# State copies moved from GpSimd to ScalarE, products written one column beside the scan, and one more unit on GpSimd

## The chip, the cores and the metric

The kernel runs on one core of one Trainium2 chip. The time is device time in microseconds (us) for the whole program. A core has five engines that each work through their own queue in order: TensorE (PE, matrix products), VectorE (DVE), ScalarE (ACT), GpSimd (POOL) and SyncE (SP, which here only starts DMA transfers). They wait for each other by semaphores, so an instruction that waits holds up all that stands behind it on its engine.

## The reference, cut to what matters

Two layers work on 8 images of 64 channels and 128 x 128 pixels. The first is an adaptive 3 x 3 filter. The second is a block with two bidirectional selective scans (Mamba) and a convolutional feed-forward part. The scans carry this change. For one direction of one block, in the reference's terms:

```
dt  = softplus(dt)
dA  = exp(einsum('bdl,dn->bldn', dt, A))          # 128 channels d, 16 states n
dBu = einsum('bdl,bnl,bdl->bldn', dt, Bm, u)
h[l] = dA[l] * h[l-1] + dBu[l]                    # along the 16384 pixels l
y   = einsum('bldn,bnl->bdl', h, Cm) + D * u
```

Each image runs it four times: block 0 forward, block 0 backward, block 1 backward, block 1 forward.

## The kernel before, in words

**Chunks and units.** The 16384 pixels are cut into 16 chunks of T = 1024. An image is four passes of 16 chunks (forward, backward, backward, forward; `d` is 0 for forward and 1 for backward), so 512 chunks in all. The first pass over a block (passes 1 and 3 of an image, `second` false) stores its y to memory; the second pass (2 and 4, `second` true) adds that y, multiplies by the gate and projects. A chunk has 128 channels x 16 states = 2048 rows, that is U = 16 units of 128 rows. Units go in pairs k = 0 to 7, unit u = 2k + i.

**What one unit costs each engine.** ScalarE makes the decay `w = exp(...)` in PSUM (`decay`, L1194; two buffers, so unit u takes the buffer of unit u-2). GpSimd makes the drive `bu` for a pair at a time (`drive`, L1186, 2048 columns, four buffers). VectorE runs `tensor_tensor_scan` (`scan`, L1212 forward, L1214 backward, the latter with all operands reversed). Its start value is one column of `state`, 16 columns that hold the last h of every unit. Then h is multiplied by C (`product`), the last h is kept in `state` for the next chunk, and TensorE sums each pair over the states into one PSUM bank `y` (`collect`, L1244 to L1251).

**Who multiplies.** `on_pool(u)` decides. It holds for even units but 4 and 12, so for u = 0, 2, 6, 8, 10, 14; a unit that meets a block of GELUs on ScalarE (`gelu_times`, 112 times in the program, always unit 6 or 14) is left out. For these units the scan writes into the SBUF tile `hs`, GpSimd copies the last column to `state` (L1231) and then multiplies in place (L1232). For the other units the scan writes over `w`, VectorE multiplies into `hs` (L1235) and ScalarE copies the last column of `w` to `state` (L1236). `hs` has four buffers of two units.

**Order.** Nothing is scheduled automatically. `plan` puts every call at a time step (one step is one scan, b is the chunk's first) and a phase (FEED, SCAN, MID, PROD, EXP, DECAY, REST), and the calls are made in that order; each engine's queue follows. The scan of unit u is at b+u, a product on VectorE at b+u PROD, one on GpSimd at b+u+1 FEED, the decay of unit u at b+u-2 EXP, the drive of pair k at b+2k-5 REST, the sum of pair k at b+2k+3 REST (one later for k = 0 and 4). In a first pass the `y` bank is copied out by ScalarE (`y_out`, L1268) at b+8h+11 DECAY for h = 0 and 1, and stored by SP (`store_y`, L1271) a step later; the next sum that needs the bank is at b+12 REST (k = 4) or at the next chunk's b+4 REST (k = 0).

**Work of other stages** is spread over the same steps: the adaptive filter of the next image (Front: `weight` L594, `weighted` L598, `softmax` L567 and L575) from about the fourth chunk of pass 3 through pass 4, a mixing stage (`times` L815, `plus` L818) through the first 11 chunks of pass 1, the feed-forward part (L892, L898, L946 to L956) from there through pass 2 into pass 3. The first image has its own filter beside its pass 1, the last has no next image's filter but its own mixing and feed-forward at the end.

Of the kernel before, what the change touches and what calls it, by code (L numbers as in the profile page):

```python
# [8 lines left out]
F32 = mybir.dt.float32  # L9
BF16 = mybir.dt.bfloat16  # L10
AF = mybir.ActivationFunctionType
ALU = mybir.AluOpType
# [3 lines left out]
P = 128  # L16
# [14 lines left out]
T = 1024  # L31
# [3 lines left out]
U = G * G  # L35
PW = W + 2
FEED, SCAN, MID, PROD, EXP, DECAY, REST = range(7)
# [18 lines left out]
def kernel(ctx: ExitStack, tc: tile.TileContext, a: dict, out: bass.AP):  # L56
# [6 lines left out]
    nc = tc.nc  # L63
# [124 lines left out]
    with tc.tile_pool(name="wspill", bufs=1) as fp, tc.tile_pool(name="wprep", bufs=2) as pp, \  # L188
            tc.tile_pool(name="wps", bufs=4, space=PSUM) as pps:
        with tc.manual_schedule():  # L190
# [106 lines left out]
            for k in range(9):  # L297
                i, j = divmod(k, 3)
# [23 lines left out]
            for (g, c0, r0, n), fn, fdn in parts:  # L322
# [7 lines left out]
                for k in range(9):  # L330
                    i, j = divmod(k, 3)
# [22 lines left out]
            for l in range(DEPTH):  # L354
# [9 lines left out]
                for d in range(2):  # L364
                    cw, xdt, xbc, dtn, al, dp = dirs[2 * l + d]
                    taps = by_taps(inx2, cw, DI, KC)
                    for j in range(KC):
                        t = turned(taps[:, j, :], ident, P, DI)
                        at = j if d == 0 else KC - 1 - j
# [39 lines left out]
    def at(time, phase, fn, *args):  # L409
        steps.setdefault((time, phase), []).append((fn, args))  # L410

    inp = ctx.enter_context(tc.tile_pool(name="in", bufs=2))
    wk = ctx.enter_context(tc.tile_pool(name="wk", bufs=2))
# [442 lines left out]
    class Ffn:  # L856
# [57 lines left out]
                    )  # L914

        def before_taps_out(self):
            self.pre = wk.tile([P, 2, T], F32, tag="hs", name="f1", bufs=4)
            for i, bank in enumerate(self.banks):
                lo = 3 * PW * (i % 2)
                nc.scalar.copy(self.pre[:, i // 2, lo : lo + 3 * PW], bank[:, 0 : 3 * PW])  # L920
# [99 lines left out]
    gelu_times = {IMAGE * b + FFN_AT + FFN_STEP * c + GELU for b in range(B - 1) for c in range(NCH)}  # L1020
# [7 lines left out]
    class Chunk:  # L1028


        def __init__(self, i):
            self.b, self.l, self.d, self.t, self.second = order[i]
            self.i, self.t0 = i, U * i
            self.first = i % NT == 0
            self.pairs = PAIRS[i % 2]
            r, last = self.t0 % IMAGE, self.b == B - 1
            self.beside_front = (
                FRONT_AT - FRONT_STEP <= r < FRONT_AT + NCH * FRONT_STEP + 16 and not last
            ) or self.t0 < FIRST_FRONT_AT + (NCH - ALONE) * FRONT_STEP + 16
            self.prev = None  # L1040
            self.bus, self.hss, self.ws = {}, {}, {}
            self.dup, self.dtp, self.bp, self.cp, self.yv = {}, {}, {}, {}, {}
            self.norm = Norm()

# [127 lines left out]
        def on_pool(self, u):  # L1172


            if u % 2 or u % 8 == 4 or self.t0 + u - 1 in gelu_times:
                return False
            return True

        def over_pair(self, what, k):
            j = self.pairs[k][0]  # L1180
# [18 lines left out]
        def scan(self, u):  # L1199
            k, i = divmod(u, 2)  # L1200
            if u == 0:
                if self.first:
                    self.state = wk.tile([P, U], F32, tag="state", name="state")
                    nc.vector.memset(self.state, 0.0)
                else:
                    self.state = self.prev.state
            if i == 0:
                self.hss[k] = wk.tile([P, 2, T], F32, tag="hs", name="hs", bufs=4)
            w, hs, bu, s0 = self.ws.pop(u), self.hss[k][:, i, :], self.bus[k][:, i, :], self.column(u)
            to = hs if self.on_pool(u) else w  # L1210
            if self.d == 0:
                nc.vector.tensor_tensor_scan(to, w, bu, s0, ALU.mult, ALU.add)  # L1212
            else:
                nc.vector.tensor_tensor_scan(to[:, ::-1], w[:, ::-1], bu[:, ::-1], s0, ALU.mult, ALU.add)  # L1214
            if not self.on_pool(u):
                self.ws[u] = w

        def column(self, u):
            (j, gp), i = self.pairs[u // 2], u % 2
# [5 lines left out]

        def product(self, u):
            k, i = divmod(u, 2)
            j, hs = self.pairs[k][0], self.hss[k][:, i, :]
            c = self.cp[j // 2][:, j % 2, :]
            if self.on_pool(u):  # L1230
                nc.gpsimd.tensor_copy(self.column(u), self.last(hs))  # L1231
                nc.gpsimd.tensor_tensor(hs, hs, c, ALU.mult)  # L1232
            else:
                w = self.ws.pop(u)
                nc.vector.tensor_tensor(hs, w, c, ALU.mult)  # L1235
                nc.scalar.copy(self.column(u), self.last(w))  # L1236

        def collect(self, k):

            hs, gp = self.hss.pop(k), self.pairs[k][1]  # L1240
            if k % 4 == 0:
                self.y = py.tile([P, N], F32, tag="y", name="y")
                for h, s in enumerate(halves):
                    nc.tensor.matmul(  # L1244
                        self.y[C * h : C * h + C, :], dskip[:, self.l, self.d, C * gp : C * gp + C], self.xc[:, s],
                        start=True, stop=False,
                    )
            for h, s in enumerate(halves):
                for i in range(2):
                    lo = C * h + 32 * i  # L1250
                    nc.tensor.matmul(  # L1251
                        self.y[lo : lo + 32, :], sel_y, hs[:, i, s], start=False, stop=(k % 4 == 3)
                    )
# [58 lines left out]
        def plan(self):  # L1312
            b = self.t0 - 2 * U

            def feed(t, fn, *args):
                if self.beside_front:
                    at(t, FEED, fn, *args)
                else:
                    at(t - 1, REST, fn, *args)

            at(b + 3, REST, self.load_hn)
            for h in range(2):
                feed(b + 7 + h, self.conv, h)
                at(b + 7 + h, DECAY, self.conv_out, h)
                if self.second:
                    feed(b + 9 + h, self.gate, h)
                    at(b + 9 + h, DECAY, self.gate_out, h)
                feed(b + 14 + h, self.step, h)
                at(b + 14 + h, DECAY, self.step_out, h)
            at(b + SILU, REST, self.silu)  # L1330
            at(b + SOFTPLUS, REST, self.softplus)
            if self.second:
                at(b + 13, REST, self.store_gate)
            b = self.t0
            feed(b - 16, self.bc)
            at(b - 16, DECAY, self.bc_out)
            at(b - 14, REST, self.store_bc)
            at(b - 13, REST, self.store_dt)
            at(b - 11, FEED, self.dtx)
            at(b - 10, REST, self.store_du)  # L1340
            j0 = self.pairs[0][0] // 2
            at(b - 10, REST, self.load_states, "bp", j0)
            at(b - 8, REST, self.load_channels, "dup", 0)
            at(b - 6, REST, self.load_channels, "dtp", 0)
            at(b - 5, REST, self.load_states, "bp", 1 - j0)
            at(b - 4, REST, self.load_states, "cp", j0)
            at(b - 3, REST, self.load_channels, "dup", 1)
            at(b - 2, REST, self.load_channels, "dtp", 1)
            at(b - 1, REST, self.load_states, "cp", 1 - j0)
            for k in range(U // 2):  # L1350
                at(b + 2 * k - 5, REST, self.drive, k)
                at(b + 2 * k + 3 + (k % 4 == 0), REST, self.collect, k)
            for u in range(U):
                at(b + u - 2, EXP, self.decay, u)
                at(b + u, SCAN, self.scan, u)
                at(b + u + self.on_pool(u), FEED if self.on_pool(u) else PROD, self.product, u)
            for h in range(2):
                if self.second:
                    at(b + 8 * h + 1, REST, self.load_yf, h)
                    at(b + 8 * h + 6, REST, self.add_yf)  # L1360
                    at(b + 8 * h + 7, REST, self.load_gate, h)
                if self.second:
                    at(b + 8 * h + 11, MID, self.y_out, h)
                else:
                    at(b + 8 * h + 11, DECAY, self.y_out, h)
                    at(b + 8 * h + 12, REST, self.store_y, h)
            if not self.second:
                return
            b += U
            n = self.norm  # L1370
            at(b + 2, REST, self.load_h)
            feed(b + 5, self.project)
            at(b + 6, DECAY, self.residual)
            at(b + 6, DECAY, self.square)
            if self.l == 0:
                at(b + 7, REST, self.store_h)
            feed(b + 12, lambda: n.means(mm_tile, self.sq))
            at(b + 13, DECAY, n.means_out)
            feed(b + 17, n.spread, mm_tile)
            at(b + 19, MID, self.normed)  # L1380
            if self.l:
                at(b + 20, DECAY, self.weighted)
            at(b + 20, REST, self.store_hn)
# [48 lines left out]
```

## Time and profile before

| | |
|---|---|
| median of 3 runs | 28777.77 us (28775.38 to 28782.68) |
| the profiled execution, its own time | 28791.63 us |
| its span on the page | 28789.8 us, mean granted TensorE clock 0.874 |
| scans on VectorE | 8192 of 2344 ns |
| drives on GpSimd | 4096 of 4534 ns |
| products on GpSimd / on VectorE | 2960 of 2352 ns / 5232 of 1222 ns |
| state copies on GpSimd / on ScalarE | 2960 of 186 ns / 5232 of 158 ns |
| du on GpSimd (L1142) | 512 of 2361 ns |

All further numbers are from this one profiled execution. Durations overlap a little from one instruction to the next, so where the text needs what an instruction really takes of its engine, it uses the distance from its start to the next start in the timeline. A memset of `state` (L1204) stands at the first scan of each pass, so its 32 starts cut the span into 32 passes: the third image's passes run from 7429 to 8293, 9150, 10012 and 10920 us, the first image's from 405 to 1285, 2144, 3014 and 3928 us, the last two passes of all from 26643 to 27487 and 28358 us.

### The profile page before, as it was taken

What the parts mean: (1) busy time and instruction counts of PE and PEld (TensorE: products, weight loads), DVE (VectorE), ACT (ScalarE), POOL (GpSimd) and SP (SyncE); (2) the same over time, 40 slices, a digit from 0 to 9 for tenths busy, and PEclk for the clock granted to TensorE, in tenths of its full rate; (3) what the DMA queues carried; (4) which work ended last, traced back from release to release, by engine and by line L of the source; (5) the groups of instructions that cost most, each with busy time, mean ns of one, the idle gap of its engine ahead of it and who ended that gap; (6) DMA issues with size and microseconds to landing.
All of it is one profiled execution on the core that took longest, in us unless ns stands there. A gap on an engine that the chain in (4) does not pass through costs nothing. (4 is left out here: it accounts for less than half of the span.)

```text
span 28789.8 us, 311790 instructions
## 1 busy us (share of the span) xinstructions
PE 22950.3 (80%) x97708; PEld 7231.1 (25%) x97708; DVE 27022.6 (94%) x17438; ACT 18537.2 (64%) x26170; POOL 27203.7 (94%) x11052
## 2 busy tenths in 40 slices
PE   7666888878788787887878788787887878878578
PEld 3112322223222232222322222222222222222123
DVE  6999999999999999999999999999999999999997
ACT  4666666666666666666666666666666666666663
POOL 4999999999999999999999999999999999999993
PEclk7777889989899888998989888898888988889789
DMA  5777787777877678776777777777777777777674
GB/s 157 226 237 222 237 254 239 247 224 238 257 238 249 223 235 259 239 243 227 241 251 244 234 233 245 245 249 231 233 250 239 252 226 236 251 240 251 203 249 140
DMA packets 2592499, 6762.78 MB, mean 235 GB/s; under 512 B 431494, under 2 KB 737046, under 8 KB 2589686
## 3 DMA queue, kind: packets, MB, share of 16 engines
q1 hardware_dynamic: 2589958, 6742.69, 72.4%
q8 instruction: 774, 12.68, 0.2%
q14 instruction: 887, 7.27, 0.1%
q10 hardware_dynamic: 880, 0.14, 0.0%
HBM read 5509.49 MB, written 1265.19 MB: 235 GB/s over the span
## 5 line engine op out<-in xcount | busy, mean ns | idle before, releaser
L1186 POOL TENSOR_TENSOR bu<-dup,bp 128x2048 f32<-128x2048 f32 x4096 | 18545.7, 4534 | 30.2 <-DMA hn_dram<-hn 11.6
L1194 ACT ACTIVATE w<-dtp,a_neg 128x1024 f32<-128x1024 f32 x8192 | 9159.5, 1119 | 1621.1 <-DVE hs L1214 704.6
L1232 POOL TENSOR_TENSOR hs<-hs,cp 128x1024 f32<-128x1024 f32 x2960 | 6963.0, 2352 | 250.9 <-DMA cp<-bc_dram 12.6
L1235 DVE TENSOR_TENSOR hs<-w,cp 128x1024 f32<-128x1024 f32 x5232 | 6394.6, 1222 | 302.3 <-DMA cp<-bc_dram 127.2
L1214 DVE TENSOR_TENSOR_SCAN w<-w,state,bu 128x1024 f32<-128x1024 f32 x2651 | 6214.8, 2344 | 119.7 <-ACT w L1194 92.4
L1212 DVE TENSOR_TENSOR_SCAN w<-w,state,bu 128x1024 f32<-128x1024 f32 x2581 | 6052.5, 2345 | 176.0 <-ACT w L1194 145.9
L1251 PE MATMUL y<-hs,sel_y 128*32 128x512 f32 x32768 | 4976.6, 687 | 678.1 <-POOL hs L1232 677.1
L1236 ACT COPY state<-w 128x1 f32<-128x1 f32 x5232 | 828.3, 158 | 5555.8 <-DVE hs L1235 5494.1
L1212 DVE TENSOR_TENSOR_SCAN hs<-w,state,bu 128x1024 f32<-128x1024 f32 x1515 | 3549.7, 2343 | 171.1 <-ACT state L1236 68.6
L1214 DVE TENSOR_TENSOR_SCAN hs<-w,state,bu 128x1024 f32<-128x1024 f32 x1445 | 3385.7, 2343 | 145.9 <-ACT state L1236 68.6
L1061 PE MATMUL xp<-hn,wx 128*128 128x512 f32 x4096 | 2345.9, 701 | 780.0 <-ACT xc L1067 317.3
L892 PE MATMUL fp<-fw,bgw 128*128 128x512 f32 (+1 forms) x5760 | 2196.4, 625 | 222.7 <-DMA fw<-xn_dram 214.6
L1244 PE MATMUL y<-xc,dskip 128*64 128x512 f32 x4096 | 1445.3, 792 | 1109.9 <-ACT yv L1268 955.9
L1103 PE MATMUL dp<-xc,wdt 128*128 128x512 f32 x2048 | 1322.7, 732 | 586.6 <-ACT dt L1110 267.6
L1251 PEld LDWEIGHTS y<-hs,sel_y 128*32 128x32 f32 x32768 | 715.4, 115 | 4228.9 <-issue 2387.4
L68 ACT ACT_TABLE_LOAD x1137 | 1458.8, 1283 | 20.8 <-PEq L1421 0.7
L1067 ACT ACTIVATE xc<-xp,cbias 128x512 f32<-128x512 f32 x1024 | 697.7, 681 | 1180.2 <-PE xp L1061 1176.3
L898 PE MATMUL fp<-fw,bgw 64*128 64x512 f32 (+1 forms) x5760 | 1383.4, 607 | 0.0
L1061 PEld LDWEIGHTS xp<-hn,wx 128*128 128x128 f32 x4096 | 799.8, 213 | 2192.5 <-issue 878.2
L609 PE MATMUL acc<-t,ident 128*128 128x512 f32 x2160 | 1332.8, 705 | 0.7 <-DVE t L598 0.7
L1142 POOL TENSOR_TENSOR du<-dt,xc 128x1024 f32<-128x1024 f32 x512 | 1208.7, 2361 | 49.6 <-ACT dt L1116 49.6
L594 PE MATMUL wb<-wt,sel_k 65*128 65x512 bf16 x1152 | 502.0, 437 | 909.4 <-DVE t L598 782.1
(211 smaller groups left out, 24911.1 us busy)
## 6 DMA issues: line engine op xcount, KB each, us to landing
bp<-bc_dram SPq DMA_DIRECT2D x4096, 256.0 KB, 3.9
dup<-du_dram SPq DMA_DIRECT2D x4096, 256.0 KB, 5.2
dtp<-dt_dram SPq DMA_DIRECT2D x4096, 256.0 KB, 5.1
cp<-bc_dram SPq DMA_DIRECT2D x4096, 256.0 KB, 4.8
hn<-hn_dram SPq DMA_DIRECT2D x1024, 256.5 KB, 4.5
dt_dram<-dt SPq DMA_DIRECT2D x512, 512.0 KB, 2.9
du_dram<-du SPq DMA_DIRECT2D x512, 512.0 KB, 2.6
yf_dram<-yv SPq DMA_DIRECT2D x512, 256.0 KB, 4.6
```

The lines of the kernel that those rows point to most:

```text
L68: nc.scalar.preload_act_table_set("natural_log_exp_and_others")
L892: nc.tensor.matmul(o, wpair[:, i, g, m], self.win[h][:, i : i + ROWS, 0:W], start=(i == 0), stop=False)
L898: nc.tensor.matmul(o, wlast[rows, i, g, m], self.win[h][rows, i : i + ROWS, lo : W + lo], start=False, stop=(i == 2),)
L1061: nc.tensor.matmul(self.xp[h], wx[:, self.l, self.d, i, :], self.hn2[:, s.start + 2 * i : s.stop + 2 * i], start=(i == 0), stop=(i == 1),)
L1186: nc.gpsimd.tensor_tensor(bu, self.dup[self.pairs[k][1]], self.over_pair("bp", k), ALU.mult)
L1194: nc.scalar.activation(w, self.dtp[gp][:, i, :], AF.Exp, scale=a_neg[:, self.l, self.d, g, j : j + 1])
L1212: nc.vector.tensor_tensor_scan(to, w, bu, s0, ALU.mult, ALU.add)
L1214: nc.vector.tensor_tensor_scan(to[:, ::-1], w[:, ::-1], bu[:, ::-1], s0, ALU.mult, ALU.add)
L1232: nc.gpsimd.tensor_tensor(hs, hs, c, ALU.mult)
L1235: nc.vector.tensor_tensor(hs, w, c, ALU.mult)
L1244: nc.tensor.matmul(self.y[C * h : C * h + C, :], dskip[:, self.l, self.d, C * gp : C * gp + C], self.xc[:, s], start=True, stop=False,)
L1251: nc.tensor.matmul(self.y[lo : lo + 32, :], sel_y, hs[:, i, s], start=False, stop=(k % 4 == 3))
```

## The change

The tile `hs` gets one column more (T + 1). On GpSimd's units the scan writes columns 1 to T in a forward pass and 0 to T-1 in a backward one; the product goes to columns 0 to T-1 or 1 to T, so it is in place but one column beside. The column with the last h is not overwritten, and ScalarE copies it to `state` (`keep`) where GpSimd did. In backward passes the product on GpSimd has all operands reversed, as the scan has. `on_pool` gives GpSimd unit 12 also, in first passes only. There the copy and the store of `y` move one step later.

```diff
-            if u % 2 or u % 8 == 4 or self.t0 + u - 1 in gelu_times:
+            if u % 2 or u == 4 or self.t0 + u - 1 in gelu_times:
                 return False
-            return True
+            return u != 12 or not self.second
...
-                self.hss[k] = wk.tile([P, 2, T], F32, tag="hs", name="hs", bufs=4)
-            w, hs, bu, s0 = self.ws.pop(u), self.hss[k][:, i, :], self.bus[k][:, i, :], self.column(u)
-            to = hs if self.on_pool(u) else w
+                self.hss[k] = wk.tile([P, 2, T + 1], F32, tag="hs", name="hs", bufs=4)
+            w, bu, s0 = self.ws.pop(u), self.bus[k][:, i, :], self.column(u)
+            to = self.hss[k][:, i, 1 - self.d : 1 - self.d + T] if self.on_pool(u) else w
+            self.hs[u] = to
...
         def product(self, u):
             k, i = divmod(u, 2)
-            j, hs = self.pairs[k][0], self.hss[k][:, i, :]
-            c = self.cp[j // 2][:, j % 2, :]
-            if self.on_pool(u):
-                nc.gpsimd.tensor_copy(self.column(u), self.last(hs))
-                nc.gpsimd.tensor_tensor(hs, hs, c, ALU.mult)
+            j = self.pairs[k][0]
+            out, hs, c = self.hss[k][:, i, self.d : self.d + T], self.hs[u], self.cp[j // 2][:, j % 2, :]
+            if not self.on_pool(u):
+                nc.vector.tensor_tensor(out, hs, c, ALU.mult)
+            elif self.d == 0:
+                nc.gpsimd.tensor_tensor(out, hs, c, ALU.mult)
             else:
-                w = self.ws.pop(u)
-                nc.vector.tensor_tensor(hs, w, c, ALU.mult)
-                nc.scalar.copy(self.column(u), self.last(w))
+                nc.gpsimd.tensor_tensor(out[:, ::-1], hs[:, ::-1], c[:, ::-1], ALU.mult)
+
+        def keep(self, u):
+            nc.scalar.copy(self.column(u), self.last(self.hs.pop(u)))
...
+            for u in range(U):
+                at(b + u + self.on_pool(u), EXP if self.on_pool(u) else PROD, self.keep, u)
...
-                    at(b + 8 * h + 11, DECAY, self.y_out, h)
-                    at(b + 8 * h + 12, REST, self.store_y, h)
+                    at(b + 8 * h + 12, DECAY, self.y_out, h)
+                    at(b + 8 * h + 13, REST, self.store_y, h)
```

`collect` reads `hs` at the shifted columns, and the feed-forward tile that shares the `hs` buffers is declared one column longer; nothing else changes.

More of the change, by code (lines that the diff above doesn't have):

```diff
@@ L916, in before_taps_out @@
         def before_taps_out(self):
-            self.pre = wk.tile([P, 2, T], F32, tag="hs", name="f1", bufs=4)
+            self.pre = wk.tile([P, 2, T + 1], F32, tag="hs", name="f1", bufs=4)
             for i, bank in enumerate(self.banks):
@@ L1040, in __init__ @@
             self.prev = None
-            self.bus, self.hss, self.ws = {}, {}, {}
+            self.bus, self.hss, self.hs, self.ws = {}, {}, {}, {}
             self.dup, self.dtp, self.bp, self.cp, self.yv = {}, {}, {}, {}, {}
@@ L1214, in scan @@
                 nc.vector.tensor_tensor_scan(to[:, ::-1], w[:, ::-1], bu[:, ::-1], s0, ALU.mult, ALU.add)
-            if not self.on_pool(u):
-                self.ws[u] = w
         def column(self, u):
@@ L1227, in product @@
             k, i = divmod(u, 2)
-            j, hs = self.pairs[k][0], self.hss[k][:, i, :]
-            c = self.cp[j // 2][:, j % 2, :]
-            if self.on_pool(u):
-                nc.gpsimd.tensor_copy(self.column(u), self.last(hs))
-                nc.gpsimd.tensor_tensor(hs, hs, c, ALU.mult)
-            else:
-                w = self.ws.pop(u)
-                nc.vector.tensor_tensor(hs, w, c, ALU.mult)
-                nc.scalar.copy(self.column(u), self.last(w))
+            j = self.pairs[k][0]
[4 more added lines that the diff above has]
+                nc.gpsimd.tensor_tensor(out, hs, c, ALU.mult)
+            else:
+                nc.gpsimd.tensor_tensor(out[:, ::-1], hs[:, ::-1], c[:, ::-1], ALU.mult)
+        def keep(self, u):
+            nc.scalar.copy(self.column(u), self.last(self.hs.pop(u)))
         def collect(self, k):
-            hs, gp = self.hss.pop(k), self.pairs[k][1]
+            hs, gp = self.hss.pop(k)[:, :, self.d : self.d + T], self.pairs[k][1]
             if k % 4 == 0:
```

## The prediction

> **What bounds the kernel now.** The page's busy line comes first: the share of each engine over the whole span.
>
> ```profile
> PE 22950.3 (80%) x97708; PEld 7231.1 (25%) x97708; DVE 27022.6 (94%) x17438; ACT 18537.2 (64%) x26170; POOL 27203.7 (94%) x11052
> ```
>
> VectorE and GpSimd tie at 94%, so the average does not say which one is the limit. The change treats first and second passes differently, so I read the busy time pass by pass. The stretches below are the first image's first two passes, the third image's four, and the last pass of all; columns are the length, then busy us (and instructions) of PE, its weight loads, DVE, ACT and POOL, the clock, the DMA share and GB/s.
>
> ```profile
> 405.00:1285.00 880.00, 640.24 (x2644) 204.97 (x2644) 840.02 (x547) 568.73 (x818) 849.72 (x356) 0.77 0.69 222
> 1285.00:2144.00 859.00, 548.15 (x2034) 153.72 (x2034) 800.93 (x463) 525.07 (x697) 851.24 (x339) 0.77 0.72 238
> 7429.00:8293.00 864.00, 672.30 (x2842) 181.34 (x2844) 804.53 (x461) 553.40 (x749) 856.56 (x344) 0.87 0.76 246
> 8293.00:9150.00 857.00, 756.41 (x3153) 235.47 (x3149) 832.14 (x508) 583.92 (x793) 829.38 (x317) 0.96 0.74 248
> 9150.00:10012.00 862.00, 642.11 (x2730) 200.24 (x2730) 833.30 (x542) 566.92 (x809) 849.93 (x355) 0.85 0.71 227
> 10012.00:10920.00 908.00, 762.84 (x3550) 274.97 (x3550) 869.02 (x609) 612.12 (x917) 856.57 (x363) 0.90 0.75 243
> 27487.00:28358.00 871.00, 689.43 (x2969) 203.75 (x2970) 806.75 (x483) 542.16 (x757) 849.89 (x346) 0.87 0.78 251
> ```
>
> To know whether the rest of POOL's time is free, I look at its timeline (start, length, engine, line, operation):
>
> ```profile
> 10026.10 0.20 POOL L1231 COPY state<-hs 128x1 f32<-128x1 f32 x1
> 10026.38 2.36 POOL L1232 TENSOR_TENSOR hs<-hs,cp 128x1024 f32<-128x1024 f32 x1
> 10028.70 4.51 POOL L1186 TENSOR_TENSOR bu<-dup,bp 128x2048 f32<-128x2048 f32 x1
> 10033.16 0.18 POOL L1231 COPY state<-hs 128x1 f32<-128x1 f32 x1
> ```
>
> From start to start a copy takes 0.27 us (0.19 of work, then 0.08 until the product that waits for it starts), a product 2.31, a drive 4.47. A full chunk is 8 x 4.47 + 6 x (0.27 + 2.31) + 2.31 for du = 53.55 us; a pass lasts 864/16 = 54.0 with the mixing stage's few additions. The pause of 0.08 after 96 copies is 7.7 us a pass: 856.56 + 7.7 = 864.3, all of 7429 to 8293. **GpSimd is full in that first pass.** The third pass is 849.9 + 7.4 and 4.7 us of DMA waits: also full. In the second passes it waits for VectorE:
>
> ```profile
> POOL state L1231 <- DVE hs L1214: 20.7, 10, 3.7
> ...
> POOL state L1231 <- DVE hs L1212: 19.9, 18, 3.3
> POOL lg L567 <- DVE sm L564: 8.4, 4, 2.1
> POOL lg L575 <- ACT sp L571: 7.8, 4, 2.0
> POOL state L1231 <- PE acc L609: 7.5, 2, 3.8
> ```
>
> (POOL's waits from 8293 to 9150, then from 10012 to 10920: total us, times, longest.) The second pass loses 20.7 us so, the fourth 43.6. There VectorE, with its own waits for ScalarE and TensorE, is the limit. The later images repeat this. Exceptions: the first image's pass 1 (POOL waits 22.4 us), its pass 2 (851.24 + 7.7 = 859, no wait: full) and the last pass (849.89 + 7.7, 11.8 us of waits: nearly full).
>
> **The change, part by part.**
>
> *GpSimd's copies go.* In a chunk 6 x 0.27 = 1.62 us less of POOL (the 112 units left out at GELUs could change the whole by at most 112 x 0.27 = 30 us, which I neglect).
>
> *Unit 12 of first passes comes.* One more product, +2.31 us of POOL. A first-pass chunk so changes by 2.31 - 1.62 = **+0.69 us**. VectorE loses a product: scan into w, product, next scan took 2.38 + 1.14 from start to start; a scan into hs takes 2.26, so -1.26 us a chunk. In a first pass that falls on an engine that is not the limit (804.5 busy of 864) and buys nothing, while POOL has no cover for its 0.69. Fifteen of the sixteen first passes are full: 15 x 16 x 0.69 = 166 us. In the first image's pass 1 POOL's waits of 1.4 us a chunk absorb some; I take 0.3 x 16 = 5. **Together +171 us.**
>
> *Second passes.* POOL loses 1.62 us a chunk (less where a unit is left out). Where it was full (two passes) I take -1.0 of the 1.62, since VectorE there waits for the gate's load and others once it is held less: 2 x 16 x 1.0 = -32 us. In the other fourteen POOL already waits; being earlier helps only where its lateness passes through TensorE to VectorE (PE y waits 677 us for POOL's hs in all). Bounds: nothing, to 1.0 us a chunk, which is about all of VectorE's listed waits in the second pass (20.2 us, 1.26 a chunk). I take -0.15: 14 x 16 x 0.15 = **-34 us**.
>
> *State copies on ScalarE.* ScalarE now makes all 8192, 2960 more of 158 ns, 0.19 with the step to the next: 2960 x 0.19 / 512 = 1.1 us a chunk. The program gives them no wait of their own, since a decay in front of each has waited for the scan already. ScalarE is idle 18 to 19 us a chunk, most of it until VectorE's product ends, and that hides them. Where ScalarE is the late one (behind table loads; VectorE waited 24 times in the second pass for its decays and copies) the copy delays the next decay by 0.19: 24 x 0.19 / 16 = 0.3 us a chunk at most. I take nothing, and keep 0.3 x 224 = 67 us for the range.
>
> *The product beside the scan, and reversed.* No row of GpSimd is shifted or reversed. In place (2352) and not in place (du, 2361) it costs the same, and VectorE's scans forward and backward are both 2343 to 2345 ns; by these it costs nothing more. The far end is GpSimd's dearest row by element, 322 ns for 72 (L575), 4.5 ns each against 2.3: +2.2 us for each of some 1600 reversed products. Below nothing there is no step to skip. I take zero: the reversed scan is the same operands turned.
>
> [...]
>
> *y one step later.* TensorE waits 955.9 us for yv (L1268) in 512 evictions. One scan step (864/256 = 3.4 us) later this grows by up to 512 x 3.4 = 1740 us, 6.8 a chunk. TensorE is idle 12 us a chunk in first passes. Behind the waiting matmul stand the filter's spread weights (L594) and the next chunk's convolutions; VectorE waits for the former (4.1 us in the third pass, longest 1.2). Two such a chunk would be 2.4 us, less than the 3.7 that VectorE has there ((862 - 833)/16 + 1.26 + 0.69). Nothing, then. On SP the store moves behind the first half of cp and ahead of the second halves of dup and dtp, which are issued some six steps (20 us) before their use and land in about 5. Nothing.
>
> *The odd column.* TensorE reads windows at odd columns already (L466, 631 ns, against 647 for L461): nothing.
>
> **Sum.** 171 - 32 - 34 = +105 us. The profiled execution's own 28791.6 would become 28,897; the median of the runs shown is 14 us under it, so **28,885**.
>
> **The rivals.** A measurement of this kernel can tell about 0.2%, 58 us, from no change.
>
> 1. *The forecast*: first passes pay 0.69 a chunk, second passes return little. +58 to +300, chance 0.60.
> 2. *Faster: the second passes follow GpSimd after all.* Its earlier products feed the sums on TensorE, these the spread weights and so VectorE. At 1.6 a chunk in all 256 chunks: 171 - 410 = -239, that is 28,539. For it: VectorE's 18.9 us of waits for L594 in the fourth pass. Against: POOL waits for VectorE there, and has done its product early as it is. It breaks even at 171/256 = 0.67 us a chunk, and is clearly faster from 0.9. Chance 0.12.
> 3. *Between them*, 0.44 to 0.9 us a chunk: within 0.2%. Chance 0.16.
> 4. *Reversed products are dear.* At the far end pass 3 chunks gain 7 x 2.2 = 15.4 and pass 2 chunks 6 x 2.2 less the 1.6 saved and 1.3 of waits = 10.3: 128 x 25.7 = 3290 us, 32,070; at a quarter of that price pass 3 gives 3.9 and pass 2 0.4, +550 us. Chance 0.12.
>
> That the change doesn't do what it says I leave out: the program has 3216 products and no copies on GpSimd.
>
> **Range.** Low: second passes at 1.0 a chunk in fourteen and 1.6 in two, 171 - 224 - 51 = -104: 28,670. High: 171 + 67 with no gain elsewhere is +238, and 1% on GpSimd's 3216 products is 76: 29,090. Outside are rival 4 and the better half of rival 2, some 0.18. Faster 0.12, same 0.16, slower 0.72.
>
> **What will show it.** GpSimd's product still 2352 ns forward and backward. First passes near 875 us with POOL without waits for VectorE; second passes within 5 us of before, POOL's waits for VectorE up by some 20 us each. PE y waiting for yv well over 1000 us, DVE's waits for L594 hardly more. I am wrong if a reversed product is longer, if second passes shorten by over 10 us each, or if first passes do not lengthen.

## The result, and the profile after

| | median | runs |
|---|---|---|
| kernel before | 28780.22 us | 28775.38 to 28783.03, 4 runs |
| changed kernel | 29241.75 us | 29227.52 to 29248.62, 4 runs |
| ratio | 1.016 | 95% interval 1.0142 to 1.0178 |

The change makes the kernel slower, as forecast, but by 461 us where 105 were forecast; the time lies above the range. First the busy line of the page:

```profile
PE 22728.0 (78%) x97708; PEld 7178.5 (25%) x97708; DVE 26757.7 (92%) x17182; ACT 18783.2 (64%) x29130; POOL 27312.3 (93%) x8348
```

No engine became the limit: all shares fell or stayed. So again pass by pass; here the third image's first and third pass of the changed kernel, between their L1204 starts (columns as before; the stretches given ahead of the prediction begin some 12 us behind the L1204 starts of the kernel before, and their lengths are right to 3 us):

```profile
7517.00:8389.00 872.00, 664.74 (x2818) 180.54 (x2820) 785.68 (x444) 556.63 (x837) 872.00 (x265) 0.86 0.75 242
9257.00:10160.00 903.00, 624.73 (x2737) 194.36 (x2735) 816.96 (x527) 570.38 (x893) 875.46 (x279) 0.83 0.69 217
```

The first pass is full of GpSimd, as forecast, and 8 us longer. The third was 862 and is 903 us, and there **neither GpSimd (875) nor VectorE (817) is full**: something makes both wait. The same cut over all images, in us against the kernel before, by groups of passes:

| passes | after |
|---|---|
| first passes without the filter (pass 1 of images 2 to 8, pass 3 of image 8) | +57 |
| first passes with the filter beside (pass 1 of image 1, pass 3 of images 1 to 7) | **+310** |
| second passes with the feed-forward part (pass 2) | +24 |
| second passes of block 1 (pass 4) | +61 |

The waits of ScalarE in that third pass (total us, times, longest), before:

```profile
ACT state L1236 <- DVE hs L1235: 179.9, 105, 4.8
...
ACT dt L1110 <- PE dp L1103: 9.0, 7, 2.4
```

and after:

```profile
ACT state L1237 <- DVE hs L1230: 159.4, 83, 6.7
ACT dt L1110 <- PE dp L1103: 57.6, 18, 6.5
```

ScalarE now waits 57.6 us instead of 9.0 for the matmuls that make the next chunk's dt (into the PSUM tile dp). One such wait, seen on TensorE's timeline of the changed kernel:

```profile
9793.24 1.05 PE L466 MATMUL hp<-xa,bgw 64*32 64x512 f32 x4
9799.59 1.98 PE L1245 MATMUL y<-xc,dskip 128*64 128x512 f32 x4 [5.30 <-ACT state L1237]
9801.50 1.93 PE L1252 MATMUL y<-hs,sel_y 128*32 128x512 f32 x8
9803.35 1.09 PE L504 MATMUL rb<-ident,r 128*64 128x128 f32 x16
9804.38 1.05 PE L461 MATMUL hp<-xa,bgw 128*32 128x512 f32 x4
9805.36 1.05 PE L466 MATMUL hp<-xa,bgw 64*32 64x512 f32 x4
9806.34 1.06 PE L1252 MATMUL y<-hs,sel_y 128*32 128x512 f32 x8
9807.33 1.12 PE L1103 MATMUL dp<-xc,wdt 128*128 128x512 f32 x2
```

and on ScalarE's and VectorE's (one fence each):

```profile
9798.96 0.58 ACT L1269 COPY yv<-y 128x512 f32<-128x512 f32 x1
...
9801.50 1.12 ACT L1194 ACTIVATE w<-dtp,a_neg 128x1024 f32<-128x1024 f32 x1 [0.49 <-DVE hs L1215]
9808.50 0.69 ACT L1110 ACTIVATE dt<-dp,dtb 128x512 f32<-128x512 f32 x1 [5.88 <-DMA dtp<-dt_dram]
9809.08 0.80 ACT L633 ACTIVATE hc<-hc,v_norm_b,v_norm_w 128x512 f32<-128x512 f32 x1
...
9811.11 1.12 ACT L1194 ACTIVATE w<-dtp,a_neg 128x1024 f32<-128x1024 f32 x1
```

```profile
9804.50 0.69 DVE L629 TENSOR_TENSOR hc<-hc,rb 128x512 f32<-128x512 f32 x1 [3.03 <-PE rb L504]
9805.10 2.35 DVE L1215 TENSOR_TENSOR_SCAN w<-w,state,bu 128x1024 f32<-128x1024 f32 x1
...
9812.26 2.36 DVE L1215 TENSOR_TENSOR_SCAN w<-w,state,bu 128x1024 f32<-128x1024 f32 x1 [1.29 <-ACT w L1194]
```

Read from the top: TensorE stands 5.30 us until y (L1269, 9798.96) is copied out to yv in SBUF; the line names the state copy right behind it. Then TensorE works off what stood behind: the sums, the filter's norm (rb) and convolution, and only at 9807.33 dp. VectorE waited 3.03 us for rb; ScalarE stood 5.88 us until the first dp ended (the line names a DMA that landed about then, but the instruction reads dp and a constant alone, and dp's end at 9808.45 fits), and the decays behind it were late: VectorE waits another 1.29 us for the one that starts at 9811.11. In the whole program TensorE's waits in front of this sum are, before:

```profile
PE y L1244 <- ACT yv L1268: 955.9, 233, 15.5
```

and after:

```profile
PE y L1245 <- ACT yv L1269: 1511.7, 293, 19.9
PE y L1245 <- ACT state L1237: 1007.5, 173, 13.3
```

The second row is put down to the state copies around yv; before, it was 34.8 us. ScalarE's wait for dp grows from 336.4 to 973.4.

### The profile page after: what moved, and what is told of

It reads as the page before. It is cut to its first block, busy times and chain, and to the rows that moved or that the text cites. A ratio compares the mean times of both kernels' runs of the same rounds, so it can differ in the third digit from the quotient of the medians.

```text
span 29225.7 us, 310698 instructions
## 1 busy us (share of the span) xinstructions
PE 22728.0 (78%) x97708; PEld 7178.5 (25%) x97708; DVE 26757.7 (92%) x17182; ACT 18783.2 (64%) x29130; POOL 27312.3 (93%) x8348
## 5 line engine op out<-in xcount | busy, mean ns | idle before, releaser
L1186 POOL TENSOR_TENSOR bu<-dup,bp 128x2048 f32<-128x2048 f32 x4096 | 18744.0, 4583 | 31.3 <-DMA hn_dram<-hn 11.6
L1230 DVE TENSOR_TENSOR hs<-w,cp 128x1024 f32<-128x1024 f32 x4976 | 6081.1, 1222 | 223.9 <-DMA cp<-bc_dram 86.0
L1215 DVE TENSOR_TENSOR_SCAN w<-w,state,bu 128x1024 f32<-128x1024 f32 x2523 | 5911.2, 2343 | 227.5 <-ACT w L1194 192.3
L1213 DVE TENSOR_TENSOR_SCAN w<-w,state,bu 128x1024 f32<-128x1024 f32 x2453 | 5747.3, 2343 | 199.9 <-ACT w L1194 188.0
L1232 POOL TENSOR_TENSOR hs<-hs,cp 128x1024 f32<-128x1024 f32 x1643 | 3993.2, 2430 | 461.8 <-DVE hs L1213 248.1
L1234 POOL TENSOR_TENSOR hs<-hs,cp 128x1024 f32<-128x1024 f32 x1573 | 3751.6, 2385 | 456.3 <-DVE hs L1215 266.1
L1213 DVE TENSOR_TENSOR_SCAN hs<-w,state,bu 128x1024 f32<-128x1024 f32 x1643 | 3851.6, 2344 | 261.7 <-ACT w L1194 168.9
L1215 DVE TENSOR_TENSOR_SCAN hs<-w,state,bu 128x1024 f32<-128x1024 f32 x1573 | 3685.7, 2343 | 223.6 <-ACT w L1194 114.0
L1245 PE MATMUL y<-xc,dskip 128*64 128x512 f32 x4096 | 1571.3, 856 | 2628.5 <-ACT yv L1269 1511.7
L1061 PE MATMUL xp<-hn,wx 128*128 128x512 f32 x4096 | 2267.2, 681 | 657.8 <-ACT sq L1294 331.7
L1103 PE MATMUL dp<-xc,wdt 128*128 128x512 f32 x2048 | 1224.4, 682 | 463.5 <-ACT state L1237 202.4
L1110 ACT ACTIVATE dt<-dp,dtb 128x512 f32<-128x512 f32 x1024 | 695.8, 680 | 1054.5 <-PE dp L1103 973.4
```

Of the source, the lines that this page charges most:

```text
L1061: nc.tensor.matmul(self.xp[h], wx[:, self.l, self.d, i, :], self.hn2[:, s.start + 2 * i : s.stop + 2 * i], start=(i == 0), stop=(i == 1),)
L1186: nc.gpsimd.tensor_tensor(bu, self.dup[self.pairs[k][1]], self.over_pair("bp", k), ALU.mult)
L1230: nc.vector.tensor_tensor(out, hs, c, ALU.mult)
L1232: nc.gpsimd.tensor_tensor(out, hs, c, ALU.mult)
L1234: nc.gpsimd.tensor_tensor(out[:, ::-1], hs[:, ::-1], c[:, ::-1], ALU.mult)
L1245: nc.tensor.matmul(self.y[C * h : C * h + C, :], dskip[:, self.l, self.d, C * gp : C * gp + C], self.xc[:, s], start=True, stop=False,)
```

## The experiments

The experiments ran on three chips (e1 to e4; e5 and e7 to e9; e6 and e10), on each of which the kernel before takes 28,752 to 28,755 us. Ratios, and times given with a sign, are against the kernel before on the same chip. The group columns are differences to the profile of the kernel before in us; there 15 us say nothing. That profile was a run of 28,792 us, so the groups of a row add up to 9 to 43 us less than the difference of the medians.

| kernel | median | ratio to before, 95% | first, no filter | first, filter | pass 2 | pass 4 |
|---|---|---|---|---|---|---|
| after (for comparison) | 29241.75 | 1.0142 to 1.0178 | +57 | +310 | +24 | +61 |
| e1: y at the old steps | 28924.34 | 1.0044 to 1.0078 | +56 | +42 | +26 | +23 |
| e2: copies only | 28566.10 | 0.9921 to 0.9951 | -152 | -59 | -31 | +21 |
| e3: y late only | 29148.31 | 1.0121 to 1.0152 | +21 | +310 | +9 | +25 |
| e4: unit 12 only | 29341.89 | 1.019 to 1.022 | +290 | +245 | +21 | -3 |
| e5: copies in idle time | 28512.16 | 0.9899 to 0.9929 | -149 | -69 | -47 | -20 |
| e7: y late, first half | 29017.37 | 1.0076 to 1.0106 | +16 | +212 | +7 | +4 |
| e8: y late, second half | 28857.10 | 1.0021 to 1.0046 | -3 | +55 | +6 | +16 |
| e9: copies, y early | 28678.28 | 0.9965 to 0.9983 | -145 | +12 | +11 | +32 |
| e6: unit 12 in second passes | 28518.77 | 0.9904 to 0.9933 | -123 | -51 | -77 | -6 |
| e10: unit 12 in some fourth passes | 28494.21 | 0.9894 to 0.9927 | -145 | -64 | -54 | -26 |

**e1, y back at the old steps.**

```diff
-                    at(b + 8 * h + 12, DECAY, self.y_out, h)
-                    at(b + 8 * h + 13, REST, self.store_y, h)
+                    at(b + 8 * h + 11, DECAY, self.y_out, h)
+                    at(b + 8 * h + 12, REST, self.store_y, h)
```

> The changed kernel with one edit undone: in first passes y is evicted and stored at the old steps (b+8h+11 and b+8h+12). Theory A (the later eviction holds TensorE's queue, and with it the filter's spread weights and the next chunk's dt, where the filter runs beside a first pass): the eight first passes with the filter, which grew by 2.0 to 2.6 us a chunk, come back to about +0.7 to +0.9 over the kernel before, so 8 x 16 x 1.8 = 230 us less: about 29,010 us; TensorE's wait for yv falls from 1512 us to near 1000. Theory B (the later eviction is covered as predicted, and it is the extra product on GpSimd that comes too late for the sums in those passes): 29,200 to 29,260, those passes stay at 56.4 us a chunk.

Measured +172 us over before instead of +461. The passes with the filter fall from +310 to +42, more than expected: theory A holds, B falls.

**e2, the copies alone.** e1, and unit 12 stays on VectorE:

```diff
-            if u % 2 or u == 4 or self.t0 + u - 1 in gelu_times:
+            if u % 2 or u % 8 == 4 or self.t0 + u - 1 in gelu_times:
                 return False
-            return u != 12 or not self.second
+            return True
```

> Only the move of the state copies to ScalarE and the product one column beside: unit 12 stays on VectorE, y is evicted at the old steps. GpSimd has 6 x 0.27 = 1.6 us a chunk less than before. If GpSimd is the limit of first passes without the filter (seven first passes and the last image's third), these shorten by 1.0 to 1.6 us a chunk; second passes tell what the copies cost on ScalarE. Theory A with copies that are hidden: second passes as before, 28,780 - 8 x 16 x 1.3 - some 40 = about 28,570. Theory C (the copies delay ScalarE's decays): second passes stay 0.4 to 0.55 us a chunk longer, as in the changed kernel, +105 us, and first passes with the filter also: about 28,700. If the total is 28,780 or more, moving the copies is no gain by itself.

186 us faster than before, as the first case expected. First passes without the filter gain 1.2 us a chunk. Unit 12 then costs e1 - e2 = 358 us.

**e3, y late alone.** The kernel before with the last two lines of the change (b+8h+12, b+8h+13).

> The kernel before with one edit: in first passes y is evicted and stored one step later. Theory A: the first passes with the filter grow by about 1.8 us a chunk, the others hardly: 28,780 + 8 x 16 x 1.8 = about 29,010 us. Theory B: within 40 us of 28,780.

+396 us, nearly twice what theory A expected, with no change on GpSimd at all. TensorE waits 2302.1 us for yv.

**e4, unit 12 alone.** The kernel before with the change's two lines of `on_pool`.

> The kernel before with one edit: GpSimd also takes unit 12 of first passes, with its own state copy as before; y is evicted at the old steps. By the sum of start-to-start distances a first-pass chunk gets 2.31 + 0.27 = 2.58 us more of GpSimd, which is full there: 15 x 16 x 2.58 + 10 = about +630, 29,410 us. If VectorE were the limit of first passes instead, it would be faster by up to 1.26 us a chunk. Theory B: the passes with the filter grow by more than 2.6 us a chunk, since the sums on TensorE wait for the late product.

+589 us against some 630: GpSimd's sum of distances holds in the main, and the passes with the filter do not grow by more than the others.

**e5, the copies in idle time.** e2 with one word changed, so that a copy stands before the one that waits for VectorE's product and not behind the next decay:

```diff
-                at(b + u + self.on_pool(u), EXP if self.on_pool(u) else PROD, self.keep, u)
+                at(b + u + self.on_pool(u), PROD, self.keep, u)
```

> The copies-only kernel (28,566 us), with the state copies of GpSimd's units one phase earlier (PROD instead of EXP of the step after the scan), so that they stand in front of the copy that waits for VectorE's product, in time in which ScalarE is idle. Theory C (a copy in front of other work delays ScalarE's next decay by 0.19 us each time ScalarE is late): 0.1 to 0.3 us a chunk less, 28,410 to 28,510. If ScalarE's copies are hidden where they are: within 30 us of 28,566.

54 us less than e2, near the lower edge of theory C's effect, nearly all of it in second passes. The intervals of the two ratios overlap, and the two kernels ran on different chips, so the place of the copies probably costs this, not surely.

**e7 and e8, y late for one half.** The kernel before:

```diff
-                    at(b + 8 * h + 11, DECAY, self.y_out, h)
-                    at(b + 8 * h + 12, REST, self.store_y, h)
+                    at(b + 8 * h + 11 + (h == 0), DECAY, self.y_out, h)
+                    at(b + 8 * h + 12 + (h == 0), REST, self.store_y, h)
```

(e8 with `h == 1`.)

> The kernel before, y of first passes evicted and stored one step later for the first half of a chunk (h = 0, step 12) alone. Both halves cost +394 us. Theory A1 (the path is the next chunk's dt: its matmuls stand at steps 14 and 15, right behind the sum that waits for the eviction at step 12, ScalarE waits for them, and its decays behind): this half carries most, +280 to +390 us. Theory A2 (the path is the filter's spread weights, which stand behind either half alike): +150 to +230 us.

> The kernel before, y of first passes evicted and stored one step later for the second half (h = 1, step 4 of the next chunk) alone. Theory A1: only the convolutions of steps 7 and 8 follow, three steps later: under +110 us. Theory A2: +150 to +230 us.

+263 and +103 us. The first half is a little under A1's bounds and over A2's, the second within A1's alone. So the two halves are not alike, as A2 has it. The lists of waits of ScalarE and VectorE in the third image's third pass, for e7:

```profile
ACT dt L1110 <- PE dp L1103: 61.3, 20, 5.6
```

```profile
DVE hc L629 <- PE rb L504: 20.2, 7, 3.9
DVE w L1214 <- ACT w L1194: 13.0, 13, 3.6
```

and for e8:

```profile
ACT dt L1110 <- PE dp L1103: 4.3, 3, 2.4
```

```profile
DVE hc L629 <- PE rb L504: 2.7, 4, 1.4
DVE w L1214 <- ACT w L1194: 1.7, 3, 0.7
```

The first half alone brings the whole wait for dt, the second none. But it also brings a wait that neither theory named: VectorE waits 20.2 us for the filter's norm (rb), which in the kernel before has no row in this pass, and that is more than the 11.4 us by which its wait for ScalarE's decays in that row grew (from 1.6). Both stand behind the same held sum. In the stretch of the changed kernel shown above the decay, and so dt, came last; which of the two costs more in all, no run separates.

**e9, y a step early.** e2 with b+8h+10 and b+8h+11.

> The copies-only kernel with y of first passes evicted and stored one step earlier (b+8h+10, b+8h+11). Theory A: TensorE's wait for yv (1084 us) falls by half or more and first passes with the filter shorten by some 0.5 us a chunk: about 28,500 us. The other way: the last sum into the bank is at b+8h+9 and waits for products, so ScalarE, with its decays behind, waits for the sum instead: 28,600 us or more.

112 us slower than e2. TensorE's wait for yv falls to 231 us, as theory A has it, but the time goes the other way. ScalarE now waits for the last sum:

```profile
ACT yv L1269 <- PE y L1252: 102.0, 70, 3.7
```

In e2 it never did. That wait does not explain the time, though: 92 of the 102 us lie in the first passes without the filter, which are as short as in e2 (-145 and -152). What grew are the first passes with the filter (+71 against e2) and pass 2 (+42). In the third image's third pass VectorE waits 12.1 us for the spread weights instead of 2.8; what holds them up stays open. Of the three steps tried the old one is the best.

**e6 and e10, unit 12 where GpSimd waits.** e5 with

```diff
-            return True
+            return u != 12 or self.second
```

and unit 12 out of the first condition, as in the change; e10 with `(self.second and self.beside_front)`.

> The kernel of e5 (copies on ScalarE in idle time, 28,512 us), with unit 12 on GpSimd in second passes instead of first ones. By the balance of the prediction VectorE is the limit of second passes and GpSimd has 1.6 to 5 us a chunk left there: VectorE loses 1.26 us a chunk, 14 x 16 x 0.6 to 1.2 us less, 28,240 to 28,380 us; in the passes with the feed-forward part GpSimd comes near full (51 + 2.3 of 53.8), so they give less than the fourth passes. Against: if the extra product is late for the sums and so for VectorE's own multiplication by the gate, second passes stay or grow: 28,500 or more.

> The same with unit 12 on GpSimd only in second passes beside the filter (the fourth pass of images 1 to 7), where GpSimd waits longest (5 us a chunk in the changed kernel). VectorE's relief of 1.26 us a chunk in some 14 x 7 chunks: up to 120 us less than 28,512. If the limit there is the loop of spread weights between TensorE and VectorE, not VectorE's own work: within 40 us of 28,512.

Neither can be told from e5 in its total. Part of e6's expectation came true: pass 2 of images 2 to 8 is 62 us shorter than in e5, 0.6 us a chunk. But the first image's pass 2, which was full of GpSimd before, is 32 us longer, and the first passes give back 26 and 18 us. In e10's fourth pass of the third image VectorE has 852 us of work instead of 869 in e5, and the pass takes 914 instead of 908: VectorE's own work does not set it. e5, e6 and e10 beat the kernel before by 0.8 to 0.9%.

## Why the prediction was wrong, point by point

**The step that failed** is "*y one step later* ... Nothing, then." It was right that TensorE would wait longer and nearly for how long (up to 1740 us more; with e3 it is 1346 in the row for yv and 322 in that for the copies around it). Wrong was what I set against it. I compared a chunk's idle time on TensorE with the added wait, and looked at one follower, the spread weights. But a queue that stands 3.4 us longer delays everything behind it: in the stretch above dp started 7.74 us after the held sum. I had named the next chunk's convolutions and not asked who waits for dt: ScalarE does, in order, with the decays of all scans behind it. The filter's norm I had not named at all, and VectorE itself waits for that. In e3's third pass of the third image these waits are 57.8 and 26.4 us, up to 7.0 and 3.9 at a time, against a slack of VectorE that was 3.7 us a chunk only on average. Measured: e3 alone +396; taking it out of the change brings +461 to +172, so -289. How these split between dt and the norm stays open.

**GpSimd's copies go, unit 12 comes: +171.** The mechanism was right, the size too large. In e1, which is the change without the later y, first passes are +98. The copies gave 1.2 us a chunk and not 1.62 where GpSimd is full (these passes have 740 copies in 128 chunks, 5.8 and not 6, which makes it 1.56), and unit 12 took 1.6 (e1 less e2: 208 us in 128 chunks) and not 2.31. In e4 the same sum, 2.58, came out at 2.27 (290 us in 128 chunks). Part of unit 12's rest is work that falls behind the end of the pass: between the L1204 starts of such a pass GpSimd works on 127 drives in e1 and on 128 or 129 in e2, up to two drives or 9 us less. That time comes back in the next pass, as the next paragraph shows.

**Second passes: -34 and -32.** Wrong in sign: +49 in e1. e2 without unit 12 has -10, so most comes with unit 12 of the first passes. In e1 it stands at the start of the second pass, whose first two chunks take 57.0 and 55.0 us (mean of images 2 to 7) against 53.4 and 51.9 in e2: GpSimd enters them with arrears. e4, which has unit 12 without the other edits, shows it at the same place, 58.7 and 55.2 us against 54.2 and 54.5 in the kernel before.

**State copies on ScalarE: nothing, at most 67.** They probably cost 54 us (e5 against e2), within the range that I kept.

**The product beside the scan, and reversed: zero.** Right. The distance from a product to the next drive is 2.31 us forward and 2.31 to 2.32 reversed; the durations in the profile are longer than before both ways (2430 and 2385 ns), which the last section takes up.

**The rivals.** "Faster" fell: with GpSimd relieved by 1.6 us a chunk second passes do not follow it (e2: -10 us in all). Without the later eviction, as in e1, the change costs +172 of the 461; the rest was no rival of mine. The sum's +105 would then have been right to 67 us, but in part by luck: its first passes were 73 us too high (+171 against +98) and its second passes 115 us too low (-66 against +49). Two slips hardly matter: the median of the runs plus 105 is 28,883 and not 28,885, and 0.4 of the third pass's 4.7 us of "DMA waits" is a wait for VectorE.

## What to carry to other kernels

A later eviction of a PSUM bank is not a matter of the bank: write down all that stands behind the waiting matmul on TensorE until the queue has caught up, and for each piece which in-order engine waits for it and what stands behind that. A share of idle time per chunk is no cover for a wait that comes in one piece: here 12 to 14 us a chunk on TensorE did not cover evictions one step (3.4 us) later, +396 us in e3. And when a change mixes a gain with a rebalancing, price the parts alone: here, taken out of the change one after the other, the copies were worth -186 us, and the two edits that came with them +289 (y) and +358 (unit 12).

## What the runs showed of the hardware

Consecutive GpSimd instructions can overlap in the profile. In the changed kernel's first pass of the third image:

```profile
7801.07 2.55 POOL L1232 TENSOR_TENSOR hs<-hs,cp 128x1024 f32<-128x1024 f32 x1
7803.38 4.70 POOL L1186 TENSOR_TENSOR bu<-dup,bp 128x2048 f32<-128x2048 f32 x1
7807.84 2.55 POOL L1232 TENSOR_TENSOR hs<-hs,cp 128x1024 f32<-128x1024 f32 x1
```

A product lasts 2.55 us and the next instruction starts 2.31 after it; before, 2.36 and 2.31. GpSimd's busy sum rose with that (27203.7 to 27312.3 us) though it had less to do (2960 copies fewer, 256 products more), and the mean of a drive rose from 4534 to 4583 ns at nearly the same spacing (4.46 to 4.50 us around these lines; before, 4.45 to 4.50 around 10000 us). The missing copies alone do not bring this. e5 has none on GpSimd either, and at the like place of the same pass its instructions hardly overlap (a drive by 0.03 us, above by 0.24):

```profile
7625.24 2.35 POOL L1232 TENSOR_TENSOR hs<-hs,cp 128x1024 f32<-128x1024 f32 x1
7627.56 4.51 POOL L1186 TENSOR_TENSOR bu<-dup,bp 128x2048 f32<-128x2048 f32 x1
7632.04 2.34 POOL L1232 TENSOR_TENSOR hs<-hs,cp 128x1024 f32<-128x1024 f32 x1
```

Why the overlap differs between the two, no run shows. The spacing is 2.31 to 2.32 us in both: distances from start to start, not durations, are what GpSimd costs here.
